# A projection in pairs of units with mirrored halves, and the other lane's matmuls only behind a pair

## The chip, the cores and the metric

The kernel runs on one core of a Trainium2 chip. The metric is the device time of one execution in microseconds (us). Five engines work side by side, each through its own queue in order: TensorE (PE; its weight loads are shown as PEld), VectorE (DVE), ScalarE (ACT), GpSimd (POOL) and SyncE (SP, which here only issues DMAs).

## The reference, cut to what matters

Four layers run over an input of 8 images of 56 x 56 positions and 192 channels; each adds its result to its input. The change touches only the first two, which are alike:

```python
p = silu(x @ p_w.T + p_b)          # 192 -> 576 channels
q = silu(x @ q_w.T + q_b)
v = silu(x @ v_w.T + v_b)
qv = q * v
o1 = toeplitz(qv along w, a1)      # one 56-long filter per channel
o2 = toeplitz(qv along h, a2)
out = (p * (o1 + o2)) @ o_w.T + o_b
```

`x` is group-normalised first. Layer 3 is a 7 x 7 depthwise convolution with an MLP, layer 4 windowed attention.

## The kernel before, in words

All data is float32. A layer of the first two has three generators, each a Python function that issues some instructions and then yields an estimate of the TensorE time that they take:

- `tno_qv` computes the product `qv` for two pairs of images (`j0` = 0 or 2). It loads `x` in groups of 256 positions (line 240), normalises them on ACT (line 246) and cuts them into **units**: 128 positions by 512 output channels (the last of three column blocks has 128). A unit (`unit`, lines 254 to 276) multiplies in two parts. The 192 input channels are 128 + 64: part 0 uses all 128 rows of the array (called F here), part 1 has the remaining 64 channels of two images in the two halves of the rows, two matmuls side by side (called H). F and H of a unit accumulate in the same PSUM banks. Then DVE adds the bias into an SBUF tile `z` (line 272). One unit later `multiply` issues the store of the product before (line 307, on SP), the silu on ACT (line 301) and the product on POOL (line 304).
- `tno_toeplitz` applies the filters, as matmuls of 56 rows by 32 columns, eight at a time in the array (line 406). A block is 64 channels; it has 4 steps along `w` (direction 0, numbered 0 to 3 here) and 4 along `h` (direction 1, steps 4 to 7), and there are 9 blocks, so 72 steps. Each step fills two PSUM tiles, which ACT copies to a buffer `ot` (line 413; two such buffers, each for two steps). One and two steps later DVE transposes a half of it (lines 424 and 426), and for direction 1 POOL adds that half into the sum `s` (line 429) and then issues the store to DRAM (line 436). In the last block DVE does the add.
- `tno_out` computes `p`, the gate and the output projection (lines 515 to 605).

PSUM is given out as four tiles of two banks each (`bank2`), in turn, to all of these. A wide unit takes two of them, a narrow one one, a toeplitz step two.

`weave` merges the generators: a lane of `tno_qv` and `tno_out` gives the beat, and after each yield it takes as many toeplitz steps (3.2 us by their estimate) as are due by the share of the lane that is done. The order in which they are issued is the order on every engine from there on, except in the first stretch, where a scheduler has some freedom. So there are five stretches with units: units with the decay tables' small matmuls (line 180, 187); units with the toeplitz steps of the layer's first image pairs; and three stretches in which the toeplitz steps are spread over units and `tno_out` together. Between two units there was a yield, so toeplitz steps could follow any unit.

Of the kernel before, what the change touches and what calls it, by code (L numbers as in the profile page):

```python
# [38 lines left out]
def view(ap, offset, dims):  # L39

    return bass.AP(ap.tensor, ap.offset + offset, [ap.ap[0], *dims])


class Net:
# [179 lines left out]
    def tno_qv(self, L, j0, xs, gn, qv, apart=None, cols=(0, 2 * D1)):  # L224

        nc, p, inp = self.nc, self.tp, self.inp
        GT = 256
        if j0 == 0:  # L230
            self.wq = self.wqp.tile([128, 3, 2 * D1], F32, name="wq", bufs=1)
            nc.sync.dma_start(self.wq[:, 0:2], inp[f"{L}_qv"])
            nc.sync.dma_start(self.wq[:, 2], inp[f"{L}_qvb"])
        w, bias = self.wq[:, 0:2], self.wq[:, 2]

        def load(g):
            t0, n = g * GT, min(GT, T - g * GT)
            x = p.tile([128, 2, 3, GT], F32, name="t6")
            of = xs[j0 : j0 + 2, :, :, t0 : t0 + n].rearrange("j k p t -> p (j k) t")
            nc.sync.dma_start(x[:, :, :, :n].rearrange("p j k t -> p (j k) t"), of)  # L240
            return x, t0, n

        def normalize(x, t0, n, js=(0, 1)):
            for j in js:
                for k in range(3):
                    nc.scalar.activation(
                        x[:, j, k, :n],
                        x[:, j, k, :n],
                        AF.Identity,
                        bias=gn[:, j0 + j, k, 1:2],  # L250
                        scale=gn[:, j0 + j, k, 0:1],
                    )

        def unit(x, s, m, c0, n, z):


            pps = [(c, min(256, n - c), self.bank2()) for c in range(0, n, 256)]
            for part in range(2):
                for c, k, pp in pps:
                    for j in range(2):  # L260
                        for b in range(2):
                            rows = HALF[b] if part else slice(0, 128)
                            nc.tensor.matmul(  # L263
                                pp[:m, b, 256 * j : 256 * j + k],
                                x[rows, j, 2 if part else b, s : s + m],
                                w[rows, part, c0 + c : c0 + c + k],

                                start=part == 0 and j == 0,
                                stop=part == 1 and j == 1,
                            )  # L270
            for c, k, pp in pps:
                nc.vector.tensor_add(  # L272
                    z[:m, c : c + k, :],
                    view(pp[:m], 0, [[1, k], [256, 4]]),
                    view(bias[:m], c0 + c, [[1, k], [0, 4]]),
                )

        def half_unit(x, s, m, c0, n, z, j):

            pp = self.bank2()  # L280
            for part in range(2):
                for b in range(2):
                    rows = HALF[b] if part else slice(0, 128)
                    nc.tensor.matmul(
                        pp[:m, b, :n],
                        x[rows, j, 2 if part else b, s : s + m],
                        w[rows, part, c0 : c0 + n],
                        start=part == 0,
                        stop=part == 1,
                    )  # L290
            nc.vector.tensor_add(
                view(z[:m], j, [[4, n], [2, 2]]),
                view(pp[:m], 0, [[1, n], [512, 2]]),
                view(bias[:m], c0, [[1, n], [0, 2]]),
            )

        def multiply(m, n, z, at, c0):
            k = n // 128
            for f in stores:
                f()  # L300
            nc.scalar.activation(z[:m, :n, :], z[:m, :n, :], AF.Silu)  # L301
            prod = p.tile([128, 4, DC * 4], F32, name="t4")
            half = z[:m, :n, :].rearrange("p (n h c) b -> p n h (c b)", h=2, c=DC)
            nc.gpsimd.tensor_mul(prod[:m, :k], half[:, :, 0], half[:, :, 1])  # L304
            n0 = c0 // 128
            stores[:] = [
                lambda: nc.sync.dma_start(
                    qv[2 * n0 : 2 * n0 + 2 * k, at : at + m, :].rearrange("n t e -> t n e"),
                    prod[:m, :k].rearrange("p n (h e) -> p (n h) e", h=2),
                )  # L310
            ]

        stores = []
        groups = -(-T // GT)
        loaded = [load(0)]
        yield 0.0
        loaded.append(load(1))
        late = None
        if apart:
            units = []  # L320
            for g in range(2):
                x, t0, n = loaded[g]
                for s in range(0, n, 128):
                    for c0 in range(0, 2 * D1, 512):
                        k = min(512, 2 * D1 - c0)
                        z = apart.tile([128, k, 4], F32, name=f"z{len(units)}", bufs=1)
                        units.append((x, s, 128, c0, k, z, t0 + s))
            for j in range(2):
                for g in range(2):
                    normalize(*loaded[g], (j,))  # L330
                for x, s, m, c0, k, z, at in units:
                    if late is not None:
                        multiply(*late)
                    half_unit(x, s, m, c0, k, z, j)
                    if j:
                        late = (m, k, z, at, c0)
                        if len(loaded) < 4:
                            loaded.append(load(len(loaded)))
                    yield 2.7 * k / 512
            loaded = loaded[2:]  # L340
            normalize(*loaded[0])
        else:
            yield from self.all_norms()
            normalize(*loaded[0])
        for g in range(2 if apart else 0, groups):
            x, t0, n = loaded.pop(0)
            for s in range(0, n, 128):
                m = min(128, n - s)
                for c0 in range(*cols, 512):
                    k = min(512, cols[1] - c0)  # L350

                    if late is not None:
                        multiply(*late)
                    if c0 == max(cols[0], min(512, cols[1] - 512)) and s + 128 >= n and g + 1 < groups:
                        normalize(*loaded[0])
                    z = p.tile([128, 512, 4], F32, name="t8")
                    unit(x, s, m, c0, k, z)
                    late = (m, k, z, t0 + s, c0)
                    if c0 == cols[0] and s == 0 and g + 2 < groups:
                        loaded.append(load(g + 2))  # L360
                    yield 5.3 * k / 512
        multiply(*late)
        stores[0]()

# [1302 lines left out]
```

## Time and profile before

| what | value |
|---|---|
| median of three runs | 5474.94 us (5457.63 to 5475.17) |
| the profiled execution's own time | 5488.15 us |
| its span in the profile | 5486.4 us |
| mean granted TensorE clock | 0.976 |
| busy time of line 263 (units) on PE | 1300.5 us |
| busy time of line 406 (toeplitz) on PE | 506.7 us |
| DVE adds of the units, line 272 | 517.6 us in 480 |
| ACT silu, line 301, and copies, line 413 | 422.9 and 492.8 us |
| POOL product, line 304, and sum, line 429 | 525.4 and 550.6 us |

The profile is of one execution. A row of its list of groups gives a line, an engine, an operation, what is written from what, a count, the busy time, the mean of one, and then the time that the engine stood idle just before such instructions with what it waited for. Matmuls are pipelined, so a busy PE may still lose time between two of them; that is read from the starts of neighbours. All stretches with units lie in the first half of the span (96 to 2637 us).

### The profile page before, as it was taken

Reading aid. Unit: us, or ns where it says so; the run is one execution under the profiler, and the core shown is the slowest. Engines: PE = TensorE matmul, PEld = TensorE weight load, DVE = VectorE, ACT = ScalarE, POOL = GpSimd, SP = SyncE. Lnnn points to the kernel's source line nnn. Section 1 sums busy time; section 2 is a strip of 40 time slices with the busy share of each in tenths; the row PEclk is TensorE's granted clock in tenths of the full one; section 3 lists DMA queues with packets and bytes.
Section 4 is the critical chain, followed back from the end, with each engine's and each line's share of the span. In section 5 each row is a group of like instructions: output and inputs, shape, how many; then the busy total and the mean of one; then the engine's idle time right before and its main releaser. Section 6 shows DMA issues by size and latency. Waiting matters only on the chain.

```text
span 5486.4 us, 144239 instructions
## 1 busy us (share of the span) xinstructions
PE 5191.3 (95%) x64672; PEld 3825.7 (70%) x64672; DVE 2587.1 (47%) x3990; ACT 2352.7 (43%) x3113; POOL 1765.1 (32%) x1292
## 2 busy tenths in 40 slices
PE   7999898999999999999999899989999999999998
PEld 3776666777777777776777788855665444777776
DVE  6444555455555555554566322422212331566666
ACT  2344454444554454655454322242323333444443
POOL 1334756133664343545443100000001101333333
PEclk9899999999999999999999999999999999999999
DMA  8558997888786999788897666634444222444443
GB/s 285 139 143 259 300 296 261 253 282 271 240 262 172 312 313 318 267 240 278 285 326 251 203 220 233 217 125 155 146 165 120 76 66 52 80 94 107 100 98 72
DMA packets 1042521, 1108.41 MB, mean 202 GB/s; under 512 B 234256, under 2 KB 977680, under 8 KB 1027504
## 3 DMA queue, kind: packets, MB, share of 16 engines
q1 hardware_dynamic: 902960, 846.82, 51.6%
q0 software_dynamic: 38144, 200.99, 9.6%
q10 hardware_dynamic: 100800, 51.38, 3.6%
q8 instruction: 508, 8.32, 0.6%
q14 instruction: 109, 0.89, 0.1%
HBM read 735.11 MB, written 363.94 MB: 200 GB/s over the span
## 4 chain that ended last, share of the span: by engine, by line
PE 48%; DMA 4%; DVE 2%; issue 2%; POOL 1%; ACT 1%; SPq 0%; POOLq 0%; ACTq 0%; DVEq 0%
PE bank L968 6%; PE bank L829 5%; PE bank L1048 5%; PE bank L1242 4%; PE bank L263 3%; PE bank L592 3%; PE bank L1062 3%; PE bank L536 3%; PE bank L1358 2%; PE bank L1272 2%; PE bank L1189 2%; PE bank L1313 2%; PE bank L586 1%; PE bank L1332 1%; PE bank L406 1%
## 5 line engine op out<-in xcount | busy, mean ns | idle before, releaser
L263 PE MATMUL bank<-wq,t 128*128 128x256 f32 (+4 forms) x7680 | 1300.5, 377 | 93.3 <-DVE t L272 48.4
L263 PEld LDWEIGHTS bank<-wq,t 128*128 128x128 f32 (+2 forms) x7680 | 1011.5, 192 | 374.9 <-issue 101.3
L272 DVE TENSOR_TENSOR t<-bank,wq 128x1024 f32<-128x1024 f32 (+3 forms) x480 | 517.6, 1112 | 695.1 <-PE bank L263 544.3
L304 POOL TENSOR_TENSOR t<-t 128x1024 f32<-128x1024 f32 (+2 forms) x288 | 525.4, 1837 | 636.3 <-ACT t L301 390.9
L413 ACT COPY ot<-bank 128x896 f32<-128x896 f32 x576 | 492.8, 910 | 517.0 <-PE bank L406 313.5
L429 POOL TENSOR_TENSOR s<-s,ot 128x1568 f32<-128x1568 f32 x128 | 550.6, 4304 | 188.4 <-DVE ot L426 123.5
L301 ACT ACTIVATE t<-t 128x2048 f32<-128x2048 f32 (+2 forms) x288 | 422.9, 1488 | 377.9 <-DVE t L272 370.6
L406 PE MATMUL bank<-q,tm 56*32 56x224 f32 x18432 | 506.7, 355 | 33.1 <-ACT ot L413 16.3
L406 PEld LDWEIGHTS bank<-q,tm 56*32 56x32 f32 x18432 | 342.5, 106 | 159.8 <-issue 69.5
L122 POOL DMA_DIRECT2D x<-t x112 | 87.0, 777 | 1098.7 <-DVE t L601 1033.6
L560 DVE TENSOR_TENSOR t<-t,bank 128x896 f32<-128x896 f32 x224 | 242.8, 1087 | 398.8 <-ACT bank L555 340.3
L555 ACT ACTIVATE bank<-bank,wo 128x448 f32<-128x448 f32 x448 | 263.1, 606 | 388.0 <-PE bank L545 368.3
L968 PE MATMUL bank<-z,w 128*128 128x448 f32 (+1 forms) x1344 | 413.2, 555 | 3.7 <-ACT h L977 3.7
L536 PE MATMUL bank<-t,wo 128*128 128x224 f32 x1792 | 374.4, 362 | 21.2 <-ACT t L515 10.7
L536 PEld LDWEIGHTS bank<-t,wo 128*128 128x128 f32 x1792 | 336.8, 193 | 51.6 <-issue 28.3
L592 PE MATMUL bank<-t,wo 128*128 128x224 f32 x1792 | 368.9, 359 | 0.0
L592 PEld LDWEIGHTS bank<-t,wo 128*128 128x128 f32 x1792 | 329.9, 190 | 31.2 <-issue 31.2
L829 PEld LDWEIGHTS bank<-xt,cm 113*112 113x112 f32 x3072 | 315.4, 179 | 43.2 <-issue 33.5
L829 PE MATMUL bank<-xt,cm 113*112 113x108 f32 (+2 forms) x3072 | 323.7, 265 | 11.2 <-ACT h L977 6.4
L968 PEld LDWEIGHTS bank<-z,w 128*128 128x128 f32 (+1 forms) x1344 | 182.6, 189 | 208.2 <-issue 197.9
L424 DVE STREAM_TRANSPOSE s<-ot 128x1792 f32<-128x1792 f32 x144 | 292.6, 2033 | 74.4 <-DMA L_sum<-s 37.8
L127 POOL DMA_DIRECT2D x<-x x64 | 36.7, 574 | 844.9 <-DVE x L999 815.2
(149 smaller groups left out, 6961.1 us busy)
## 6 DMA issues: line engine op xcount, KB each, us to landing
q<-qv SPq DMA_DIRECT2D x36, 3584.0 KB
t<-L_sum SPq DMA_DIRECT2D x112, 1008.0 KB
L_sum<-s POOLq DMA_DIRECT2D x256, 392.0 KB, 7.3
qv<-t SPq DMA_DIRECT2D x192, 512.0 KB
cm<-in_L_cm SPq DMA_DIRECT2D x96, 896.0 KB
tm<-L_tab SPq DMA_DIRECT2D x288, 240.0 KB
q<-qv SPq DMA_DIRECT2D x40, 1568.0 KB
q<-qv ACTq DMA_DIRECT2D x32, 1568.0 KB
```

What stands on the lines that cost most here:

```text
L263: nc.tensor.matmul(pp[:m, b, 256 * j : 256 * j + k], x[rows, j, 2 if part else b, s : s + m], w[rows, part, c0 + c : c0 + c + k],  start=p ...
L272: nc.vector.tensor_add(z[:m, c : c + k, :], view(pp[:m], 0, [[1, k], [256, 4]]), view(bias[:m], c0 + c, [[1, k], [0, 4]]),)
L301: nc.scalar.activation(z[:m, :n, :], z[:m, :n, :], AF.Silu)
L304: nc.gpsimd.tensor_mul(prod[:m, :k], half[:, :, 0], half[:, :, 1])
L406: nc.tensor.matmul(pt[32 * j : 32 * j + 32, r, hf * 224 : (hf + 1) * 224], tm[rows, at : at + 32], q[rows, :, 4 * c : 4 * c + 4], start=Tr ...
L413: nc.scalar.copy(view(ot, 4 * (g % 4), [[16, 2], [32, 112], [1, 4]]), view(pt, 0, [[512, 2], [4, 112], [1, 4]]),)
L424: nc.vector.transpose(to, of.rearrange("p (i k) -> p i k", k=32))
L429: add.tensor_add(to, to, view(of, 0, [[1, 28], [32, 56]]))
L536: mm(gs[c // 2][:, b, c % 2 * 256 : c % 2 * 256 + N], pw[:, 0, 128 * c : 128 * c + 128], xn[:, b], start=c % 2 == 0, stop=False,)
L592: mm(P[:, b, :N], ow[:, c, 0:128], g[:, 4 * b + c], start=False, stop=c == 3)
L829: nc.tensor.matmul(pc[:, 128 * e + 4 * m0 : 128 * e + 4 * m1], cm[:113, e, k, :], xt[:, m0 - 1 + k : m1 - 1 + k, c + e, :], start=n == 0 a ...
L968: nc.tensor.matmul(phs[c][:, s, :TT], w0[rows, part, at : at + 128], z[rows, Z[2 if part else s], :], start=part == flip, stop=part != flip,)
```

## The change: what it does

Each generator of units keeps a flag that turns over with every unit. With the flag set, the unit issues part 1 (H) before part 0 (F); without it, as before. As the flag is turned over ahead of the first unit, units go H F, F H, H F, F H. After the first unit of such a pair the generator now yields 0, and after the second the time of both, so `weave` issues toeplitz steps (or the decay tables' work) only behind a pair.

```diff
-        def unit(x, s, m, c0, n, z):
+        def unit(x, s, m, c0, n, z, flip):
+            first, last = (1, 0) if flip else (0, 1)
...
-            for part in range(2):
+            for part in (first, last):
...
-                                start=part == 0 and j == 0,
-                                stop=part == 1 and j == 1,
+                                start=part == first and j == 0,
+                                stop=part == last and j == 1,
...
+        flip, held = False, 0.0
         for g in range(2 if apart else 0, groups):
...
-                    unit(x, s, m, c0, k, z)
+                    flip = not flip
+                    unit(x, s, m, c0, k, z, flip)
                     late = (m, k, z, t0 + s, c0)
                     if c0 == cols[0] and s == 0 and g + 2 < groups:
                         loaded.append(load(g + 2))
-                    yield 5.3 * k / 512
+                    held += 5.3 * k / 512
+                    yield 0.0 if flip else held
+                    held = held if flip else 0.0
```

## The prediction

> **What bounds the kernel now.** I read the page first (engines, then the 40 slices, then the costliest groups), then a table of the five stretches in which the projection units run, then the waits of the stretch with the largest gap, and last its timeline. From the page:
>
> ```profile
> PE 5191.3 (95%) x64672; PEld 3825.7 (70%) x64672; DVE 2587.1 (47%) x3990; ACT 2352.7 (43%) x3113; POOL 1765.1 (32%) x1292
> L263 PE MATMUL bank<-wq,t 128*128 128x256 f32 (+4 forms) x7680 | 1300.5, 377 | 93.3 <-DVE t L272 48.4
> ```
>
> The reader sees that TensorE is busy 95% of the span, and that the projections (line 263) are its largest group, 1300 of 5191 us. So time taken off TensorE is, as a rule, time taken off the end. The five stretches, named here lanes 0 to 4 (columns: length, then busy time of PE, PEld, DVE, ACT, POOL, granted clock, DMA share):
>
> ```profile
> 96.00:422.00 326.00, 300.07 (x1737) 232.96 (x1737) 148.22 (x259) 129.05 (x134) 119.95 (x91) 0.93 0.61 164
> 422.00:964.00 542.00, 473.15 (x6673) 359.75 (x6672) 290.86 (x205) 264.14 (x295) 319.63 (x190) 0.95 0.87 279
> 1347.00:1760.00 413.00, 402.18 (x4371) 312.48 (x4371) 231.11 (x187) 206.86 (x231) 230.90 (x139) 0.97 0.70 223
> 2182.00:2337.00 155.00, 149.36 (x1865) 114.73 (x1864) 95.77 (x74) 99.41 (x121) 89.45 (x49) 0.97 0.81 273
> 2337.00:2637.00 300.00, 271.88 (x3145) 208.48 (x3144) 146.60 (x117) 164.68 (x213) 166.17 (x104) 0.96 0.85 258
> ```
>
> Lanes 2 and 3 are nearly pure TensorE. Lane 1, where all 72 toeplitz steps lie among 75 units, is not: TensorE idles 69 us, and POOL is at 320 of 542 us. What ACT waits for there:
>
> ```profile
> ACT ot L413 <- POOL s L429: 120.0, 14, 16.6
> ```
>
> The price of a switch between kinds of matmul is read from the weight loads in order of time (start, length, then the group; F is 128 rows, H is 64 rows, the toeplitz step is 56 by 32):
>
> ```profile
> 436.46 3.32 PEld L263 LDWEIGHTS bank<-wq,t 128*128 128x128 f32 x16 [0.33 <-issue]
> 440.11 1.60 PEld L263 LDWEIGHTS bank<-wq,t 64*128 64x128 f32 x16 [0.33 <-issue]
> ...
> 471.26 1.60 PEld L263 LDWEIGHTS bank<-wq,t 64*128 64x128 f32 x16 [0.33 <-issue]
> 473.19 2.83 PEld L406 LDWEIGHTS bank<-q,tm 56*32 56x32 f32 x128 [0.33 <-issue]
> 476.38 3.32 PEld L263 LDWEIGHTS bank<-wq,t 128*128 128x128 f32 x16 [0.36 <-ACT ot L413]
> 480.02 1.60 PEld L263 LDWEIGHTS bank<-wq,t 64*128 64x128 f32 x16 [0.33 <-issue]
> 481.95 1.32 PEld L406 LDWEIGHTS bank<-q,tm 56*32 56x32 f32 x64 [0.33 <-issue]
> 483.63 1.61 PEld L263 LDWEIGHTS bank<-wq,t 128*128 128x128 f32 x16 [0.36 <-DVE t L272]
> ```
>
> Two toeplitz steps together take 476.38 - 473.19 = 3.19 us, one alone 483.63 - 481.95 = 1.68. The second adds 1.51, so 0.17 of the lone one is the switch. 1.51 us are 8 rounds of eight concurrent matmuls of 224 columns, 0.189 a round, thus 0.216 for 256 columns. An F half of a unit is 16 x 0.216 = 3.46 and takes 440.11 - 436.46 = 3.65; an H half is 8 x 0.216 = 1.73 and takes 473.19 - 471.26 = 1.93. A switch costs 0.17 to 0.20 us; I take 0.19.
>
> **What the Trainium skill says.** "TensorEngine Tiling (Array Packing)", section Tiling Modes, Key Properties: changing the tiling mode, not just the tile, drains the TensorE. The trace agrees and gives the size, 0.19 us. The same page, PSUM Bottleneck: tiling speeds up the TensorE but not the evacuation of PSUM; the trace shows it in lane 1, where a toeplitz step of 1.5 us needs two copies of 0.87 on ACT (1.72 a pair) and one transpose of 2.03 on DVE. "TensorE: Matmul & The Clock Gate", Part 1: after idle time of a window of about 3.4 us the clock drops to half. The trace agrees: after the first toeplitz step's 8 us wait the 128-column F half took 2.00 us (464.48 to 466.48 in the same view) against 1.09 elsewhere. So a long stall costs more than its length. The same page says that ACT and DVE are strict FIFO: a blocked copy holds the silu behind it.
>
> **The change part by part.** *Switches.* I counted them in the instruction order of both programs. Units of one generator: lane 0 159 -> 113, lane 1 201 -> 140, lane 2 184 -> 133, lane 3 67 -> 43, lane 4 125 -> 91: 216 fewer, times 0.19 = 41 us. Nothing else is added to or taken from any engine: the same matmuls, adds, silus, multiplies and DMAs. The first unit of a pair now has H first, the second H last; each has the same 16 matmuls.
>
> *What is off the path.* In lane 0 the small matmuls of the decay tables (line 180) now come two in a row at three places, each reading what DVE made of the one before. The nearest row is PE's wait of 2.7 us for `h` of line 182; with the units' adds (1.2 us each) ahead on DVE I take 2 us each, 0 to 4: +6 us. In lanes 2 to 4, about a tenth of the time is not TensorE's (clock 0.96 to 0.97 and gaps), so of 109 switches x 0.19 = 21 us I give back 2. In lane 1 about half the time is in stretches that POOL bounds (next paragraph), so half of 61 x 0.19 = 11.6 is given back: +6. That leaves 41 - 6 - 2 - 6 = 27 us.
>
> *Toeplitz steps in clusters.* The held time lets the other lane go on only behind a pair, so its steps come two or three at a time. Each step needs two of four double banks, so does a unit: the reuse distance is unchanged, and a pair fills all four. Hand replay: the first unit's adds (2.36) lie beside the second's matmuls (5.2); the second's end 1.7 us after it, when the first step has just run on the other two banks. No stall from there. The `ot` buffer is different. There are two, each for two steps. A buffer filled in steps 4 to 7 of a block (direction 1) is emptied by a transpose on DVE (2.03) and then an add on POOL (4.28), issued one and two steps later, and the copy of the step after that waits for it. So at two turns per block (step 7 to 0, step 1 to 2) a step needs what the step just before it started. The timeline of such a turn, where 7 and 0 stand together already:
>
> ```profile
> 665.55 4.28 POOL L429 TENSOR_TENSOR s<-s,ot 128x1568 f32<-128x1568 f32 x1
> 669.86 1.72 ACT L413 COPY ot<-bank 128x896 f32<-128x896 f32 x2 [11.48 <-POOL s L429]
> ...
> 670.82 3.31 PE L406 MATMUL bank<-q,tm 56*32 56x224 f32 x128 [1.25 <-ACT ot L413]
> 677.17 3.73 PE L263 MATMUL bank<-wq,t 128*128 128x128 f32 x24 [3.04 <-ACT ot L413]
> 684.70 5.56 PE L263 MATMUL bank<-wq,t 128*128 128x256 f32 x24 [3.81 <-ACT ot L413]
> ```
>
> Add on POOL, copy on ACT, then bank on PE: with the clock it lost 10 us against the ideal durations. In lane 1 before, 4 of 16 turns are adjacent and lost 10.4, 2.6, 8.9 and 10.2 us (mean 8), the 12 with a unit between lost 3 each: 68 us of the 93 that the lane is over its matmuls at these durations (410) and its switches (39); the rest of 542 is the first load and the last tail. In the changed order 10 of 16 are adjacent, 6 have a whole pair between. But each is now preceded by a pair of units, 10.4 us in which POOL clears its queue. Replayed with the durations above, an adjacent turn then costs 0.3 us (two wide units next) to 5.5 (a narrow one next: it takes the bank at once), and with a pair between, nothing. Bounds: 3 to 8 for an adjacent one, 0 to 3 for a separate one. I take 6 and 1: 66 us against 68, so -2. The other lanes get 3 more adjacent turns (5 against 2), with POOL at 56% in lane 2 and 58% in lane 3: 3 us each, +9.
>
> *SP and POOL queues.* The store of a product (line 307) is still issued one unit later, and the next loads of `q` and `tm` still behind the block's last step; a pair lasts as long as two single rounds did (13.6 against 14.5 us), so their landing stays covered. POOL waited 104 us in lane 1 for those stores, and a shift there is inside the range.
>
> Sum: -27 - 2 + 9 = -20 us, against the profiled execution's 5488.15 (span 5486.4): 5468. That execution lies 13 us above the median of the three runs, 5474.94; there the sum gives 5455. This kernel's runs spread over 0.3%, so a change under 0.5% (27 us) can't be told from none.
>
> **The rivals.** (C) *Hidden anyway*: the saved switches of all lanes turn into waits for copies and adds. For it, POOL and ACT in lane 1; against it, lanes 2 and 3 at 96 to 97% TensorE. -4 us, 5471. (A) *Pairs also relieve the turns*: adjacent ones cost 3 and separate ones 1 in lane 1, 36 us against 68, and nothing in the other lanes: -27 - 32 = -59 us, 5416. For it, the replay; against it, POOL's 13 us of adds and multiplies in a pair of 13.6. (B) *Slower, by one mechanism*: the adjacent turns, 15 instead of 6 in all, cost the 8 us that the present ones cost, since the multiplies and store issues of a pair now stand in POOL's queue together: 9 x 8 = 72, less 27, is +45 us, 5520. It decides above 27 / 9 = 3 us each, if the separate ones don't get better. For it, the four measured ones; against it, that they met a POOL with a backlog. (D) That the order isn't as described can't be: the first of each pair is the one with H first, but the number of switches is the same either way.
>
> **How the numbers follow.** Likeliest 0.38 (own range 5435 to 5475), A 0.22, B 0.27, C 0.13. The predicted time is the likeliest's, 5455. The range goes from A's end, 5412, to just short of B's, 5515. Faster by over 0.5% (under 5447.5): 0.37 of the likeliest and nearly all of A, 0.35. Slower by over 0.5% (over 5502): nine tenths of B and a little else, 0.25. Between: 0.40.
>
> **What would show it.** Right: lane 2 shorter by 8 to 10 us at an unchanged count of matmuls; the loads of two neighbouring H halves without the 0.33 between them; lane 1's wait of ACT for `s` of line 429 near 120 us. A: that wait under 80 and lane 1 under 510 us. B: over 180, with the granted clock of lane 1 below 0.95 and the stall in front of the first unit behind a cluster. Wrong in the base: lanes 2 and 3 no shorter, which would mean that the switch is not on TensorE's path.

## The result, and the profile after

| | before | after |
|---|---|---|
| median, us | 5474.94 (7 runs) | 5499.26 (7 runs) |
| ratio, 95% interval | | 1.005 [1.004, 1.006] |
| profiled execution, us | 5488.15 | 5497.01 |

The change made the kernel slower by 24 us where 20 us less were forecast; the interval, 22 to 33 us, is clear of zero. The profiles show only a part of it: the profiled execution before lies 13 us above its median, the one after 2 us below, so the two differ by 9 us. The page of the kernel after, the same two rows:

```profile
PE 5164.6 (94%) x64672; PEld 3842.6 (70%) x64672; DVE 2602.4 (47%) x3990; ACT 2352.4 (43%) x3113; POOL 1765.0 (32%) x1292
L264 PE MATMUL bank<-wq,t 64*128 64x256 f32 (+4 forms) x7680 | 1282.3, 380 | 147.0 <-ACT ot L418 60.6
```

TensorE is busy 27 us less, the units' group 18 us less, and the idle time before that group has grown from 93 to 147 us, with ACT's copies in place of DVE's adds as the main cause. So the switches did go. The weight loads in order of time show one pair behind two steps:

```profile
502.41 2.83 PEld L411 LDWEIGHTS bank<-q,tm 56*32 56x32 f32 x128
505.60 1.60 PEld L264 LDWEIGHTS bank<-wq,t 64*128 64x128 f32 x16 [0.36 <-issue]
507.52 6.77 PEld L264 LDWEIGHTS bank<-wq,t 128*128 128x128 f32 x32 [0.33 <-issue]
514.63 1.60 PEld L264 LDWEIGHTS bank<-wq,t 64*128 64x128 f32 x16 [0.33 <-issue]
516.56 4.34 PEld L411 LDWEIGHTS bank<-q,tm 56*32 56x32 f32 x192 [0.33 <-issue]
```

H, then the F halves of both units as one group of 32 without a gap, then H, then three steps: 514.63 - 507.52 = 7.11 us for 32 x 0.216 = 6.91, one switch of 0.20 for two units' F.

From the starts of neighbouring matmuls I split each lane into three parts: the matmuls at the ideal durations of the prediction, up to 0.20 us per change of kind (switches), and what is over (stalls). A lane goes from the start of its first unit to that of the next lane or the last matmul of its last unit; lane 4 runs on for 17 to 19 us past it. These bounds are not the prediction's: before the change, lane 3's units run to 2373.6 us, not to 2337. There is one profiled execution each: two of the same kernel (e4 and s3, or e7 and s4 below) differ by up to 9 us in lane 3, 7 in lane 1 and 3 in the others.

| lane | length before / after | switches before / after | stalls before / after |
|---|---|---|---|
| 0 | 334.2 / 336.3 | 27.7 / 20.3 | 37.4 / 42.6 |
| 1 | 533.2 / 537.6 | 38.3 / 28.7 | 93.2 / 107.2 |
| 2 | 393.1 / 392.2 | 34.7 / 25.3 | 15.7 / 24.2 |
| 3 | 181.4 / 193.9 | 12.4 / 8.0 | 13.6 / 30.5 |
| 4 | 263.6 / 262.0 | 24.0 / 18.0 | 29.3 / 33.5 |
| sum | 1705.5 / 1722.0 | 137.1 / 100.4 | 189.2 / 238.0 |

The saving on switches is 36.7 us, close to the 41 predicted. Stalls took 49 us more. The table has two blemishes: in lane 0 the parts leave 269 us for the matmuls before and 273 after, so 4 us there belong to neither column, and lane 4's tail holds a wait of 8.3 us before and 4.0 after, which hides a part of the growth of its stalls.

A stall in this table is not idle time alone. Lane 3 before and after (start:end, length, busy time of PE, PEld, DVE, ACT and POOL with counts, granted clock, DMA share, GB/s):

```profile
2192.20:2373.60 181.40, 171.61 (x1888) 130.27 (x1889) 109.63 (x74) 113.76 (x139) 110.18 (x65) 0.98 0.79 261
2195.70:2389.60 193.90, 175.31 (x1888) 137.43 (x1888) 112.90 (x73) 113.58 (x139) 106.20 (x64) 0.93 0.74 243
```

With 4 us of switches less, TensorE is busy 4 us longer for the same matmuls, since the clock was granted at 0.93 instead of 0.98. Over the five lanes TensorE's idle time rises from 135 to 173 us, and by my estimate from the stretches at half clock the time lost by running slower while busy rises from 54 to 67 us.

The worst single stalls have one form. This is the turn from step 1 to step 2 inside a cluster of three (timeline of the kernel after; start, length, group, and the idle time before it):

```profile
521.69 8.46 POOL L434 TENSOR_TENSOR s<-s,ot 128x1568 f32<-128x1568 f32 x2
...
530.17 1.71 ACT L418 COPY ot<-bank 128x896 f32<-128x896 f32 x2 [9.13 <-POOL s L434]
...
531.13 5.45 PE L264 MATMUL bank<-wq,t 128*128 128x256 f32 x24 [5.44 <-ACT ot L418]
```

Two adds into the sum stand on POOL back to back, the copy of the third step waits 9.1 us for the second of them, and the wide unit that follows a narrow one waits 5.4 us for the bank. That is the case that the prediction priced at 5.5 us.

### The profile page after: what moved, and what is told of

It reads as the page before. It is cut to its first block, busy times and chain, and to the rows that moved or that the text cites. A ratio compares the mean times of both kernels' runs of the same rounds, so it can differ in the third digit from the quotient of the medians.

```text
span 5495.2 us, 144206 instructions
## 1 busy us (share of the span) xinstructions
PE 5164.6 (94%) x64672; PEld 3842.6 (70%) x64672; DVE 2602.4 (47%) x3990; ACT 2352.4 (43%) x3113; POOL 1765.0 (32%) x1292
## 4 chain that ended last, share of the span: by engine, by line
PE 71%; DMA 8%; DVE 7%; POOL 4%; issue 4%; ACT 3%; SPq 2%; POOLq 0%; ACTq 0%; DVEq 0%
PE bank L264 14%; PE bank L597 6%; PE bank L973 6%; PE bank L541 6%; PE bank L834 5%; PE bank L1247 4%; PE bank L1053 4%; PE bank L411 4%; DMA qv<-t 3%; PE bank L1067 3%; PE bank L591 3%; POOL s L434 2%; PE bank L550 2%; PE bank L1363 2%; PE bank L1277 2%
## 5 line engine op out<-in xcount | busy, mean ns | idle before, releaser
L264 PE MATMUL bank<-wq,t 64*128 64x256 f32 (+4 forms) x7680 | 1282.3, 380 | 147.0 <-ACT ot L418 60.6
L264 PEld LDWEIGHTS bank<-wq,t 64*128 64x128 f32 (+2 forms) x7680 | 1024.2, 194 | 406.5 <-issue 96.6
L302 ACT ACTIVATE t<-t 128x2048 f32<-128x2048 f32 (+2 forms) x288 | 423.9, 1488 | 537.6 <-DVE t L273 522.7
L834 PE MATMUL bank<-xt,cm 113*112 113x108 f32 (+2 forms) x3072 | 324.6, 265 | 11.9 <-ACT h L982 7.4
L127 POOL DMA_DIRECT2D x<-x x64 | 36.7, 574 | 846.0 <-DVE x L1004 815.9
```

The lines of the kernel that those rows point to most:

```text
L264: nc.tensor.matmul(pp[:m, b, 256 * j : 256 * j + k], x[rows, j, 2 if part else b, s : s + m], w[rows, part, c0 + c : c0 + c + k],  start=p ...
L834: nc.tensor.matmul(pc[:, 128 * e + 4 * m0 : 128 * e + 4 * m1], cm[:113, e, k, :], xt[:, m0 - 1 + k : m1 - 1 + k, c + e, :], start=n == 0 a ...
```

## The experiments

All ratios are to the kernel before, run next to it on the same chip, with the 95% interval. Ratios of different experiments often come from different chips.

**e1: mirrored halves alone.**

```diff
-                    held += 5.3 * k / 512
-                    yield 0.0 if flip else held
-                    held = held if flip else 0.0
+                    yield 5.3 * k / 512
```

> The mirrored halves alone; every unit yields its own time again, so toeplitz steps may follow any unit as before. 610 switches instead of 736. Theory T (the loss of the change comes from the steps in clusters, the switches are worth 0.19 us each): 126 x 0.19 = 24 us less than before, ratio 0.9956, and the time above matmuls and switches in the unit stretches stays near the 194 us of before. Rival M (the mirrored order itself makes units wait, since a unit with F first holds its banks in another order): ratio 1.000 or more, and that time grows as in the changed kernel (to about 240).

Measured 5462.71 us, ratio 0.9993 [0.9985, 1.0001]: 4 us of the 24, and the interval reaches none at all. In its profile, switches fell from 137.1 to 115.7 us and stalls rose from 189.2 to 205.6. Lane 0 became clearly shorter (325.8 us against 334.2); lanes 1 to 4 moved by 2 to 7 us either way, little or no more than profiles of one kernel differ. Neither theory fits: T asked for the 24 us, M for stalls near 240.

**e2: clusters alone.**

```diff
-                    unit(x, s, m, c0, k, z, flip)
+                    unit(x, s, m, c0, k, z, False)
```

> The clusters alone: steps only behind a pair, but every unit F then H. 691 switches instead of 736, worth 9 us. Theory T: the clusters' stalls come in full (48 us in the profiles of before and after), so 39 us slower than before, ratio 1.007. Rival M: without the mirrored order no new stalls, ratio 0.998.

Measured 5510.50 us, 1.0078 [1.0065, 1.0090]: +43 us. Holding is what costs, as theory T had it. With e1 and the changed kernel this is a table of two by two: mirroring saves 4 us without holding (24 us of switches) and 15 with it (32 us); holding costs 43 us without mirroring and 31 with it, although it removes switches too (9 and 17 us).

**e3 and e4: the transpose right behind its step's copies**, in the changed kernel and in the kernel before.

```diff
-                    yield 3.2
                     behind()
+                    yield 3.2
```

> The changed kernel with the transpose (and POOL's add behind it) issued right behind a step's own copies, before the yield, instead of at the start of the next step: the ot buffer is emptied one step earlier. Theory O (the stalls of the clusters are those of the ot buffer, whose add stands in the same cluster as the copy that waits for it): the adjacent turns cost little, 30 to 45 us less than the changed kernel, ratio to before 0.997 to 1.000. Rival P (four PSUM tiles are too few for a pair plus a cluster, or the product stores land too late): within 10 us of the changed kernel, ratio 1.003 to 1.006.

> The kernel before with the same earlier transpose. Theory O: it too has turns whose add comes late (4 adjacent, 12 behind one unit, 68 us in lane 1), so 20 to 40 us less than before, ratio 0.993 to 0.996. Rival P: within 10 us of before.

Measured: e3 5465.02 us, 0.9995 [0.9987, 1.0003], about 30 us less than the changed kernel; e4 5462.22 us, 0.9993 [0.9980, 1.0005]. The earlier transpose takes back the loss in the changed kernel, as theory O forecast, and does little to the kernel before, where O had 20 to 40 us. The waits of TensorE's weight loads in lane 1 say why the second expectation fell. Kernel before:

```profile
PEld bank L263 <- ACT ot L413: 36.3, 26, 5.9
...
PEld bank L406 <- ACT ot L413: 19.3, 12, 5.2
PEld bank L406 <- DVE t L272: 6.6, 6, 3.0
```

The changed kernel:

```profile
PEld bank L264 <- ACT ot L418: 56.7, 31, 8.4
...
PEld bank L264 <- DVE t L273: 22.6, 5, 11.4
```

e3:

```profile
PEld bank L411 <- DVE t L273: 28.5, 17, 8.0
...
PEld bank L264 <- ACT ot L418: 22.0, 22, 5.0
PEld bank L264 <- DVE t L273: 17.3, 5, 10.8
```

Each row is the waiting engine and line, its releaser, the sum, the number and the longest. The wait for copies falls from 56.7 to 22.0 us in e3, but that for DVE's adds of the units rises from 22.6 + 4.2 to 28.5 + 17.3. In the order of issue the last transpose of a cluster now stands ahead of the next units' adds on DVE; that this is the cause was not tried. In part, one wait takes the place of another. In e4 the same happens: copies 17.2 + 4.5 us, adds 30.8 + 27.8. The first two blocks also show that the sum of waits for copies is the same before (36.3 + 19.3) and after (56.7); they come in fewer, longer pieces.

**e5: the pair the other way round** (F H, H F).

```diff
-            first, last = (1, 0) if flip else (0, 1)
+            first, last = (0, 1) if flip else (1, 0)
```

> The changed kernel with the pair the other way round: F H, H F. The switches stay 520, the clusters stay the same; only the unit right behind a cluster now starts with F, whose second bank is wanted 1.73 us after the first (H wants it after 0.86). Theory H (starting with H behind toeplitz steps costs, as both banks must be free sooner): 10 to 20 us less than the changed kernel, ratio 1.001 to 1.003. Rival N (the saved switches are swallowed by waits on DVE, ACT and POOL whatever the order in the unit): same as the changed kernel, ratio 1.004 to 1.006.

Measured 5503.06 us, 1.0054 [1.0041, 1.0066]: the same as the change. Theory H fell: which half stands first behind the steps made no difference that shows.

**e6 and e7: H first only behind an H**, nothing held; e7 with the early transpose too.

```diff
-                    flip = not flip
+                    flip, self.h_last = self.h_last, not self.h_last
...
-                    held += 5.3 * k / 512
-                    yield 0.0 if flip else held
-                    held = held if flip else 0.0
+                    yield 5.3 * k / 512
...
         def along(n, q, ot, g):
+            self.h_last = False
```

> No pairs held, H first only if the unit before ended in H with no toeplitz step or output projection between: the same switches saved as with the mirrored halves alone (about 126), no H first behind a step. Theory H: the 24 us come through that the mirrored halves alone turned into 4, ratio 0.995 to 0.997. Rival N: like the mirrored halves alone, ratio 0.998 to 1.000.

> The one before with the transpose issued one step earlier as well. Theory H: 0.9993 of the early transpose times 0.996, ratio 0.994 to 0.996. Rival N: 0.998 to 0.9995.

Measured: e6 5463.37 us, 0.9989 [0.9981, 0.9996], no better than e1 by more than its interval; e7 5454.19 us, 0.9965 [0.9953, 0.9978]. The second is the fastest of the study, 19 us under the kernel before. Theory H had less than 0.997 for e6, so N fits there; e7 lies between the two.

**e8: every second add of the sum on DVE**, in the changed kernel.

```diff
-                add = nc.vector if last else nc.gpsimd
+                add = nc.vector if last or hf else nc.gpsimd
```

> The changed kernel with every second add into the sum (the second half of a buffer, the one that the next copy waits for) on DVE instead of POOL: 2.9 us on DVE for 4.3 on POOL, and not behind POOL's queue. Theory O (the clusters' loss is the wait of the copy for POOL's add): 15 to 35 us less than the changed kernel, ratio 0.998 to 1.002, and ACT's wait for the sum on POOL in lane 1 from 86 us to under 30. Rival P (banks or product stores): no gain, and DVE's longer queue makes the units' adds late: ratio 1.005 or more.

Measured 5492.99 us, 1.0045 [1.0031, 1.0058]: no clear gain. What ACT waited for in lane 1, in the changed kernel and then in e8:

```profile
ACT ot L418 <- POOL s L434: 86.1, 14, 10.5
```

```profile
ACT ot L418 <- DVE s L434: 57.0, 10, 8.1
...
ACT ot L418 <- POOL s L434: 0.9, 1, 0.9
```

The wait for POOL is gone, as theory O said, but copies now wait 57 us for the add on DVE. So POOL's queue alone isn't what delays them. The transpose and the add of a turn start with the step just before; moving their start (e3) helps, moving the engine brought nothing clear. Rival P isn't excluded here: with the adds on DVE, ACT's waits for the units' adds rose too, from 103.8 to 118.7 us in lane 1, and may have eaten a gain.

**e9, e10, e11: where holding costs.** All have the mirrored halves; pairs are held everywhere but in lane 0 (e9), only in lanes 1 and 2 (e10), only in lanes 3 and 4 (e11). The edit of e9; the others differ in the condition:

```diff
-        flip, held = False, 0.0
+        flip, held, hold = False, 0.0, not apart
...
-                    yield 0.0 if flip else held
-                    held = held if flip else 0.0
+                    yield 0.0 if flip and hold else held
+                    held = held if flip and hold else 0.0
```

> The changed kernel, but pairs are not held in lane 0, where the other work is the decay tables' chain of small matmuls. Theory C (that chain, two of its steps in a row, costs what lane 0 is longer in the profiles: 336 us against 326 with the mirrored halves alone): 8 to 11 us less than the changed kernel, ratio 1.003. Rival O (all of the loss is in the turns of the ot buffer, lanes 1 and 2): no gain, 1.005.

> Mirrored halves everywhere, pairs held in lanes 1 and 2 only. Rival O: nearly all of the loss, ratio 1.003 to 1.005 (the mirrored halves alone had 0.9993). Theory S (the loss is spread as the profiles' stretches show it, lane 0 about 10 us, lanes 3 and 4 about 10, lanes 1 and 2 about 10): ratio 1.001 to 1.002.

> Mirrored halves everywhere, pairs held in lanes 3 and 4 only. Theory S: about 10 us more than the mirrored halves alone, ratio 1.001. Rival O: lanes 3 and 4 have only one or two turns more in a cluster, ratio 0.999 to 1.000.

Measured: e9 1.0034 [1.0022, 1.0047] (5496.01 us), e10 1.0014 [1.0005, 1.0023] (5483.84), e11 1.0010 [1.0004, 1.0016] (5484.23). Against e1's 0.9993 and the change's 1.005, holding costs 0.0016 in lane 0, 0.0021 in lanes 1 and 2 and 0.0017 in lanes 3 and 4: 9, 11 and 9 us, in sum 29 of the 31. Each difference has an interval about as wide as itself, and e9's just reaches zero, but theory S holds and O, all in the turns, falls.

The kept profiles agree with these places. Lane 0 with mirrored halves and no held pairs takes 324.6 to 327.7 us in four of them (e1, e9, e10, e11), with held pairs 332.3 to 336.3 in three (the change, e3, e8), and without either 330.9 to 334.2 in three (before, e4, s3; the early transpose doesn't reach lane 0). So there the mirrored halves bring their 6 us of switches in full, and holding takes 8 back. Lanes 3 and 4 together, up to the last unit, take 428.8 and 429.1 us when not held (e10, e1) and 437.4 to 440.4 when held (the change, e9, e11).

**s1 to s4: does a switch reach the end?** In s1 and s2 each wide unit does F H F H, one bank after the other; s2 also has the early transpose, s3 is e4 and s4 is e7 again, on the same chip.

```diff
-            for part in range(2):
-                for c, k, pp in pps:
+            for c, k, pp in pps:
+                for part in range(2):
```

> The kernel before with F and H of one bank before those of the other (F H F H in each wide unit): two more switches in each of 192 wide units, 384 x 0.19 = 73 us of TensorE time added. If a switch is on the path everywhere: ratio 1.013. Theory W (much of a small gain or loss of TensorE time between two waits is swallowed; the mirrored halves alone brought 4 of 24 us): well under that, 1.003 to 1.009, least in lane 1. The first bank is finished earlier, which can only help the adds.

> The same with the transpose one step earlier. Theory W: with the copies' waits gone less is swallowed, so the added switches cost more than in the kernel before: 10 us or more above that, ratio to before 1.006 to 1.012. If waits have nothing to do with it: the same difference as without the early transpose.

> The early transpose alone once more, on the same chip as the next, so that the two can be compared: 0.998 to 1.0005.

> The early transpose with H first only behind an H. Theory W: 10 to 20 us under the early transpose alone (without the early transpose the same mirrored halves brought 4 to 6), ratio to before 0.996 to 0.9975. If waits have nothing to do with it: 4 to 6 us under it.

Measured: s1 5504.62 us, 1.0049 [1.0037, 1.0061]; s2 5519.03, 1.0070 [1.0058, 1.0082]; s3 5469.29, 0.9982 [0.9975, 0.9989]; s4 5457.26, 0.9968 [0.9955, 0.9980]. 384 more switches cost 27 us at the end; with the early transpose 0.0070 - (-0.0018) = 0.0088, or 48 us, as theory W had it. The profile has the 72 us of added switches (137.1 to 209.2), so the price of 0.19 us is right. The saved switches under the early transpose (s3 to s4, 0.0014; e4 to e7, 0.0028) bring 8 and 15 us, in intervals too wide to tell from the 4 to 6 without it, so W isn't decided there. The five lanes of the kernel before, cut at the bounds of the table above:

```profile
96.70:430.90 334.20, 308.27 (x1795) 237.89 (x1793) 152.16 (x263) 130.26 (x134) 122.98 (x92) 0.93 0.61 164
430.90:964.10 533.20, 464.35 (x6611) 354.42 (x6609) 286.32 (x202) 262.23 (x294) 315.90 (x187) 0.95 0.88 280
1366.40:1759.50 393.10, 384.33 (x4112) 298.99 (x4112) 218.49 (x164) 199.16 (x220) 225.58 (x137) 0.98 0.70 223
2192.20:2373.60 181.40, 171.61 (x1888) 130.27 (x1889) 109.63 (x74) 113.76 (x139) 110.18 (x65) 0.98 0.79 261
2373.60:2637.20 263.60, 241.57 (x2969) 186.47 (x2969) 124.72 (x101) 144.91 (x188) 142.40 (x87) 0.95 0.87 262
```

and of s1:

```profile
96.80:439.20 342.40, 318.62 (x1795) 229.29 (x1793) 156.40 (x263) 130.64 (x135) 123.23 (x92) 0.94 0.60 160
439.20:973.50 534.30, 485.94 (x6610) 348.34 (x6608) 290.18 (x201) 262.26 (x295) 316.38 (x187) 0.95 0.87 280
1372.10:1782.80 410.70, 402.58 (x4112) 288.49 (x4112) 224.57 (x164) 199.19 (x220) 227.60 (x137) 0.98 0.66 214
2216.00:2402.00 186.00, 179.89 (x1888) 125.58 (x1888) 110.28 (x74) 113.79 (x139) 108.83 (x65) 0.99 0.78 253
2402.00:2664.00 262.00, 247.92 (x2969) 180.25 (x2969) 127.43 (x101) 144.41 (x188) 142.55 (x87) 0.98 0.87 264
```

Lane 1 takes 22 us more of TensorE and is 1.1 us longer: what is added to TensorE there fills its gaps. Lane 2 takes 18 us more and is 17.6 us longer: there TensorE is the path. Lanes 3 and 4 take 15 us more and are 3 us longer, lane 0 10 and 8. Against the spread between profiles of one kernel this is clear in lanes 0 to 2, and not in 3 and 4. In s2 lanes 3 and 4 do pass it on: together, up to the last unit, they take 438.0 us against 418.9 and 418.3 in e4 and s3. That is most of what lies between 27 and 48 us. One reserve: in these units the first bank is also finished earlier, so a part of the cover may be earlier adds.

## Why the prediction was wrong

The forecast was 5455 us (range 5412 to 5515). The measured time lies in the range, but the range held it because it reached almost to rival B's end, not because the sum was near: the time moved the other way. Sum and result lie 44 us apart, about 1.005 against 0.9963. The change is smaller than the 27 us below which the prediction called it invisible, yet seven runs a side told it from none.

- *Switches*: right. Price and count came out as predicted (36.7 us on TensorE against 41; s1 added 72 where 73 was computed).
- *What of it lies on the path* (the deductions that left 27 us): this step failed. Besides the 6 us for lane 0's chain it gave back 2 us in lanes 2 to 4 and half of lane 1, so it counted 33 of the 41 us as time off the end. The mirrored halves brought 4 of their 24 us without holding and 15 of 32 with it; at those shares 7 to 19 of the 41 came through, and this step is 14 to 26 of the 44 us. The busy share was read as a share of the path: lane 1 swallowed 21 of the 22 us added in s1 though TensorE is busy 87% there, and lanes 3 and 4, busy 95% and 92%, passed on 3 of 15 us in s1 and all of it in s2.
- The prediction's own sign for this was lanes 2 and 3 being no shorter. So it came: lane 2 went from 393.1 to 392.2 us and lane 3 from 181.4 to 193.9. But its reading, that the switch is not on TensorE's path, doesn't hold for lane 2, where s1 shows added switches coming through; there the saving was made and stalls grew by 8.5 us. For savings alone, e1 has lane 2 shorter by 1.8 us for 7.2 us of switches. With the early transpose it is 5 us for 7.8: 393.5 and 393.2 us in e4 and s3, 388.5 and 388.3 in e7 and s4.
- *Clusters*: the term was mis-sized, and this is the rest, 18 to 30 us of the 44. -2 us in lane 1 and +9 in the other lanes were put for the turns, and +6 for lane 0, 13 in all. Holding cost 31 to 43 us; of the 31, 9 in lane 0, 11 in lanes 1 and 2, 9 in lanes 3 and 4. In lane 1 the stall described was seen (behind a narrow unit 5.4 us where the replay had 5.5), and the earlier transpose took about 30 us of the whole back. That doesn't single out the turns, though: it brings 4 to 10 us without holding too (e4, s3), and it can't reach lane 0. And the relief that was set against it, separate turns at 1 us instead of 3, doesn't show: the waits for copies sum to the same and are longer.
- *Lane 0*: the size of 6 us was near 9, the cause was not shown. Two chained matmuls of the decay tables follow each other 0.79 us apart in the profile after (210.96 and 211.75), 0.4 of it a wait, not 2 us, and the waits of line 180's matmuls and weight loads for `h` of line 182 sum to 4.5 us after where they were 5.6. What else holding costs there wasn't found.
- *Rival B* named the right sign, and the right place in part; with its sum unmet, that is part luck. Its price, 8 us for each of nine more turns, would have given +45. Lane 1's clock fell to 0.93 and the stalls stand behind clusters, as it said, but its main sign in the profile was wrong: ACT's wait for the sum on POOL was to rise above 180 us in lane 1 and fell from 120 to 86. What rose was TensorE's stall time.
- *Lanes 3 and 4* weren't looked at for clusters beyond the 3 turns counted for lanes 2 to 4, and cost 9 us. In e11 that is shown as a place only; its mechanism was not tried. The 9 us that were put for those turns agree with it by luck, as far as is known.
- *A reading*: the wait ahead of the slow F half at 464.48 us, put at 8 us, is 5.8 us of idle TensorE in the trace. The clock at half speed behind it is right (0.50 from 461.3 to 466.5).

## What to carry to other kernels

A TensorE that is busy 90% of a stretch need not be that stretch's path. Split its starts into matmuls, switches and stalls, and test with a kernel that adds TensorE time before crediting a saving. Putting work of one lane into clusters to save switches also puts a ring buffer's producer and its next consumer next to each other; look for the wait that is a fixed number of steps back. The way to have the switches without the clusters was to choose the order of the halves by what was issued last, and to empty the ring one step earlier; neither gained much alone, together 0.9965.

## What the runs showed of the hardware

The cost of a change between kinds of float32 matmul is small and steady, 0.17 to 0.20 us for 128 rows, 64 rows and 56 by 32, in every direction that the loads shown have. Adding 384 of them to one kernel moved its time by 27 us, and the same edit moved a kernel that differs only in when a transpose is issued by 48. Stalls and clock went together: lane 3, with 9 us more of idle TensorE, was granted a mean clock of 0.93 where it had 0.98, and its matmuls kept TensorE busy for longer.
